# Two 3x3 convolutions behind an attention layer: input channels in two row halves of the array, each half summed in a PSUM bank of its own

## The chip, the cores and the metric

One core of a Trainium2 chip runs the kernel. The metric is the device time of one execution in microseconds (us). The kernel before takes 2547.97 us, the median of four runs (2547.29 to 2551.29).

## What is computed

The input `x` is float32 of shape (4, 128, 64, 64): four images of 128 channels. Two layers follow each other. The first is a group norm, a self-attention with four heads of 32 over the 4096 positions of an image, a projection and a residual. The second, which the change touches, is a block of two quantized 3x3 convolutions, each with batch-norm statistics over all images:

```python
def conv3x3_decomposed(x, wq):
    xp = jnp.pad(x, ((0, 0), (0, 0), (1, 1), (1, 1)))
    out = jnp.zeros((B, wq.shape[0], H, W), dtype=x.dtype)
    for kh in range(3):
        for kw in range(3):
            out = out + jnp.einsum('bchw,oc->bohw', xp[:, :, kh:kh + H, kw:kw + W], wq[:, :, kh, kw])
    return out
...
residual = x
out = conv3x3_decomposed(x, lsq_quantize(w1, alpha1))
out = jax.nn.relu(batchnorm(out, gamma1, beta1))
out = conv3x3_decomposed(out, lsq_quantize(w2, alpha2))
out = batchnorm(out, gamma2, beta2)
out = jax.nn.relu(out + residual)
```

Both convolutions have 128 input and 128 output channels, so one tap of one block of positions is one product of a 128x128 weight with a 128-row operand. The mean and variance of the batch norm run over all 4 x 4096 positions of a channel. The second convolution can therefore start only when the first is finished for all images.

## The kernel before

**Stages.** The attention comes first and fills about 2235 us. In it, TensorE works in bursts of three score pairs (line 442) and three weight halves (line 456), ScalarE takes the exponentials (line 444) and VectorE adds up rows (line 471). Its scores are products over 64 rows: `k[r, half, ...]` against `q[r, half, part, :]` with `r` the lower or upper 64 partitions, and the two halves go to two banks of one PSUM tile (lines 439 to 443). Then come the two convolution layers (`layer`, called in lines 885 and 939) and a closing pass that adds the residual and stores the output (lines 940 to 951).

**Bands and chunks.** An image is cut into four bands of 16 rows, which makes 16 bands for four images (`bandlist`). A band has two chunks `j` of 8 rows, that is of 512 positions, which is one PSUM bank of float32. A band's input is held three times in SBUF, padded to 18 rows of 66: `t` in float32, `hi` rounded to the fast format fp32r, and `lo`, the rest. `split` (lines 570 to 575) makes `hi` with a VectorE cast and `lo` with a VectorE subtraction. In the second layer `relu_band` (lines 898 to 903) does this after ScalarE has applied batch norm and ReLU. All come from one ring of nine buffers (`kpool`).

**One chunk.** `conv` (lines 775 to 785) issues 18 matmuls into one bank: 9 taps over `hi`, then 9 over `lo`, each with the full 128x128 weight of the tap and a moving operand of 8 rows of 64.

**PSUM.** `conv_tile` takes a tile of two banks from `pss`, a ring of three such tiles that the attention's scores also use; here one tile holds the two chunks of a band. The two remaining banks are the pool `psa`.

**Order of the work.** The order on each engine is the order of the program's text (`manual_schedule`). The first two bands of the first layer are convolved at the attention's end, among its last steps, into the tiles `early` (lines 791 to 803). `layer` (lines 834 to 861) then goes over the bands but the last: convolve both chunks, call `prepare(m)`, which prepares band m + 2 (and loads band m + 3 in the first layer), then for each chunk run `bn_stats` on VectorE and a copy on ScalarE, both reading the bank. At m = 5 of the first layer, `prepare` also counts bad values with one small matmul. The last band's chunks go to banks of `psa`; while TensorE works on them, VectorE aggregates the statistics of all other chunks (line 850), and ten small matmuls (`keep_warm`) close the layer.

Of the kernel before, what the change touches and what calls it, by code (L numbers as in the profile page):

```python
# [16 lines left out]
F32 = mybir.dt.float32  # L17
AF = mybir.ActivationFunctionType
ALU = mybir.AluOpType
# [3 lines left out]
P = 128  # L23
# [3 lines left out]
TAPS = 9  # L27
FB = 512
# [50 lines left out]
def _fast_body(ctx, tc, x, norm_w, norm_b, qkv_wt, qkv_b, proj_wt, proj_b,  # L79
               w1, alpha1, gamma1, beta1, w2, alpha2, gamma2, beta2, out, cnt):  # L80
    nc = tc.nc
    B, C, H, W = x.shape
    assert C == P and W == 64
    N = H * W
    RB = FB // W
    NB = N // FB
# [52 lines left out]
    wq = [const.tile([P, TAPS, P], F32R, name="wq0")]  # L139
# [69 lines left out]
    pss = ctx.enter_context(tc.tile_pool(name="pss", bufs=3, space=PSUM))  # L209
# [96 lines left out]
    def keep_warm(count):  # L306

        t = psa.tile([P, FB], F32, name=f"idle{count}", tag="a")
        for _ in range(count):
            nc.tensor.matmul(t[:, 0:P], gavg, gavg, start=True, stop=True)  # L310
# [266 lines left out]
    raw, ready = {}, {}  # L577
# [17 lines left out]
    st = small.tile([P, NB, 6], F32, name="st0", tag="st")  # L595
# [144 lines left out]
    todo, parts = [], {}  # L740
# [34 lines left out]
    def conv(parts, ps, j, w):  # L775
        hi, lo = parts
        r0 = j * RB
        n = 0
        for part in (hi, lo):
            for tap in range(TAPS):  # L780
                kh, kw = divmod(tap, 3)
                nc.tensor.matmul(ps.rearrange("p (r w) -> p r w", w=W), w[:, tap, :],  # L782
                                 part[:, r0 + kh : r0 + kh + RB, kw : kw + W],
                                 start=(n == 0), stop=(n == 2 * TAPS - 1))
                n += 1

    def conv_tile(i, b, g):
        return pss.tile([P, 2, FB], F32, name=f"c{i}_{b}_{g}", tag="s")


    early = [conv_tile(0, *bandlist[m]) for m in range(2)]
    last = parts[len(blocks) - 1]
    conv(ready[0, 0, 0], early[0][:, 0, :], 0, wq[0])
# [13 lines left out]
    cv = [mid.tile([P, N], F32, name=f"cv{b}") for b in range(B)]  # L807
# [11 lines left out]
    def batch_norm(i, st):  # L819

        mv = small.tile([P, 2], F32, name=f"bmv{i}", tag="mv")
        nc.vector.bn_aggr(mv, st)
        r = small.tile([P, 1], F32, name=f"br{i}", tag="rs")
        nc.vector.tensor_scalar(r, mv[:, 1:2], a_q[i], EPS, ALU.mult, ALU.add)
        nc.gpsimd.tensor_tensor(r, r, mhalf, ALU.pow)
        na = small.tile([P, 1], F32, name=f"bn{i}", tag="dv")
        nc.vector.tensor_tensor(na, r, a_n[i], ALU.mult)
        c = small.tile([P, 1], F32, name=f"bc{i}", tag="gc")
        nc.vector.scalar_tensor_tensor(c, mv[:, 0:1], na, bn[i][1], ALU.mult, ALU.add)
        a = small.tile([P, 1], F32, name=f"ba{i}", tag="ga")  # L830
        nc.vector.tensor_tensor(a, r, a_g[i], ALU.mult)
        return a, c

    def layer(i, prepare, done):


        st = mid.tile([P, B * NB, 6], F32, name=f"st{i}")
        end = mid.tile([P, 15], F32, name=f"end{i}")
        nc.gpsimd.memset(end[:, 0:1], float((B * NB - 2) * FB))
        for m, (b, g) in enumerate(bandlist[:-1]):  # L840
            ps = done[m] if m < len(done) else conv_tile(i, b, g)
            for j in range(2):
                if m >= len(done):
                    conv(ready[i, b, g], ps[:, j, :], j, wq[i])
            prepare(m)
            for j in range(2):
                c = 2 * g + j
                nc.vector.bn_stats(st[:, b * NB + c, :], ps[:, j, :])  # L848
                nc.scalar.copy(cv[b][:, c * FB : (c + 1) * FB], ps[:, j, :])  # L849
        nc.vector.bn_aggr(end[:, 1:3], st.rearrange("p j s -> p (j s)")[:, : 6 * B * NB - 12])  # L850
        nc.vector.tensor_scalar(end[:, 2:3], end[:, 2:3], float((B * NB - 2) * FB), None, ALU.mult)
        b, g = bandlist[-1]
        for j in range(2):
            ps = psa.tile([P, FB], F32, name=f"c{i}_last{j}", tag="a")
            conv(ready[i, b, g], ps, j, wq[i])
            c = 2 * g + j
            nc.vector.bn_stats(end[:, 3 + 6 * j : 9 + 6 * j], ps)
            nc.scalar.copy(cv[b][:, c * FB : (c + 1) * FB], ps)
        prepare(len(bandlist) - 1)
        keep_warm(10)  # L860
        return batch_norm(i, end)
# [11 lines left out]
    def first(m):  # L873
# [8 lines left out]
        if m + 2 < len(bandlist) and m > 0:  # L882
            split_band(*bandlist[m + 2])

    a1, c1 = layer(0, first, early)

    def relu_rows(b, g, t, r0, r1):
# [45 lines left out]
    def second(m):  # L933
        if m + 2 < len(bandlist):
            relu_band(*bandlist[m + 2])
        if m < 4 * B - 4:
            load_res(m // 4, m % 4)

    a2, c2 = layer(1, second, [])
    for i in range(4):  # L940
        load_res(B - 1, i)
    for b in range(B):
        for j in range(4):
            for p in range(2 if b == j == 0 else 1):
                n = HN // 2 if b == j == 0 else HN
                y = res[b, j][:, p * n : (p + 1) * n]
# [464 lines left out]
```

## Time and profile before

| | us |
|---|---|
| median of four runs | 2547.97 |
| the profiled execution | 2549.55 |
| its span (first to last instruction) | 2547.8 |
| TensorE busy (share of the span) | 2508.6 (98%) |
| VectorE busy | 2137.4 (84%) |
| ScalarE busy | 2087.4 (82%) |
| copy of a chunk, `cv<-c`, line 849, 128x512 | 0.587 each, 60 of them |
| `bn_stats` of a chunk, line 848, 128x512 | 0.699 each, 60 of them |
| cast to `hi`, line 573, 128x1188 | 0.764 each |
| subtraction to `lo`, line 574, 128x1188 | 1.396 each |
| sum of a PSUM and an SBUF operand, `kst<-pk,b,kst`, line 352, 128x512 | 0.751 each |

All times below are of one profiled execution, counted from its first instruction. A group of instructions is named by its line, engine, operation and tiles (out<-in). Matmuls are pipelined: the duration of one (about 0.4 us) is longer than the distance from its start to the next start, so a rate is read from starts, not from durations.

### The profile page before, as it was taken

To read this page: it belongs to the slowest core of one execution; us is meant where nothing else is said; L and a number is where in the kernel's file an instruction comes from. 1 tells how busy PE (TensorE), PEld (TensorE's weight loads), DVE (VectorE), ACT (ScalarE), POOL (GpSimd) and SP (SyncE) were. 2 spreads that over 40 slices of the span, in tenths; PEclk is the share of its full clock that TensorE was granted. 3 is DMA by queue.
4 is the path that set the end of the run, shared out by engine and by line. 5 is a ranking of instruction groups with operands and counts; after the bars stand their busy time and mean duration, and the time that the engine had idled before them with its cause. 6 is when DMAs were issued, how large, how long until landed. Compare 5 with 4: busy or idle time off the path is not lost.

```text
span 2547.8 us, 65043 instructions
## 1 busy us (share of the span) xinstructions
PE 2508.6 (98%) x28708; PEld 1505.6 (59%) x28708; DVE 2137.4 (84%) x1402; ACT 2087.4 (82%) x2278; POOL 281.6 (11%) x461
## 2 busy tenths in 40 slices
PE   9999999999999999999999999999999999999995
PEld 6555555555555555555555555555555555577774
DVE  6899888889988889889988888889999999954445
ACT  5998888999988999999988899989999999911224
POOL 2111111111011111110111111111000011000000
PEclk9999999999999999999999999999999999999998
DMA  6877667787757667797766666796666666645004
GB/s 196 190 185 171 166 171 183 174 203 177 184 132 191 168 153 171 164 230 163 172 164 171 158 165 157 191 201 152 149 138 144 146 144 152 148 89 160 1 1 166
DMA packets 148955, 403.86 MB, mean 159 GB/s; under 512 B 59417, under 2 KB 60185, under 8 KB 120121
## 3 DMA queue, kind: packets, MB, share of 16 engines
q0 software_dynamic: 45840, 280.39, 48.2%
q1 hardware_dynamic: 100952, 113.60, 16.9%
q8 instruction: 227, 3.72, 0.6%
q10 hardware_dynamic: 1872, 5.64, 0.6%
q14 instruction: 64, 0.52, 0.1%
HBM read 107.48 MB, written 56.42 MB: 64 GB/s over the span
## 4 chain that ended last, share of the span: by engine, by line
PE 70%; issue 3%; DMA 2%; DVE 1%; ACT 1%; POOL 0%; ACTq 0%; POOLq 0%; DVEq 0%
PE s L442 31%; PE acc L456 27%; PE c L782 9%; DMA rm<-p 2%; PE l L488 1%; PE po L317 1%; PE pk L317 1%; PE pq L317 1%; PE pv L317 1%; DVE r L471 0%; ACT res L949 0%; ACT p L444 0%; PE c_last L782 0%; DVE r L469 0%; DVE res L948 0%
## 5 line engine op out<-in xcount | busy, mean ns | idle before, releaser
L444 ACT ACTIVATE p<-s 128x1024 f32<-128x1024 f32 x2048 | 1950.6, 1032 | 202.8 <-PE s L442 154.2
L471 DVE TENSOR_TENSOR r<-r,p 128x2048 f32<-128x2048 f32 x768 | 1758.3, 2289 | 65.2 <-ACT p L444 14.8
L442 PE MATMUL s<-q,k 64*128 64x512 f32 x8192 | 1139.7, 410 | 2.0 <-ACT p L444 1.6
L456 PE MATMUL acc<-p,v 128*32 128x256 f32 x16384 | 1026.4, 383 | 0.0
L442 PEld LDWEIGHTS s<-q,k 64*128 64x128 f32 x8192 | 717.0, 185 | 409.9 <-issue 166.9
L456 PEld LDWEIGHTS acc<-p,v 128*32 128x32 f32 x16384 | 463.7, 109 | 482.3 <-issue 247.7
L466 POOL DMA_DIRECT2D rm<-p x160 | 139.5, 872 | 803.6 <-ACT p L444 555.0
L849 ACT COPY cv<-c 128x512 f32<-128x512 f32 x60 | 35.2, 587 | 200.1 <-DVE st L848 200.1
L782 PE MATMUL c<-hi,wq 128*128 128x512 f32 x540 | 139.1, 402 | 1.3 <-issue 1.3
L782 PE MATMUL c<-lo,wq 128*128 128x512 f32 x540 | 138.5, 401 | 0.0
L848 DVE BATCH_NORM_STATS2 st<-c 128x6 f32<-128x512 f32 x60 | 41.9, 699 | 104.0 <-PE c L782 83.4
L782 PEld LDWEIGHTS c<-hi,wq 128*128 128x128 f32 x540 | 101.3, 188 | 30.2 <-issue 2.1
L782 PEld LDWEIGHTS c<-lo,wq 128*128 128x128 f32 x540 | 101.8, 188 | 27.1
L352 DVE SCALAR_TENSOR_TENSOR kst<-pk,b,kst 128x512 fp32r<-128x512 f32 x32 | 24.0, 751 | 83.4 <-PE s L442 68.5
L469 DVE TENSOR_TENSOR r<-p,p 128x2048 f32<-128x2048 f32 x32 | 73.2, 2289 | 12.9 <-ACT p L444 12.9
L352 DVE SCALAR_TENSOR_TENSOR qst<-pq,b,qst 128x512 fp32r<-128x512 f32 x32 | 24.0, 751 | 58.4 <-PE s L442 47.4
L356 POOL DMA_DIRECT2D qd<-qst x31 | 23.6, 761 | 265.6 <-DVE qst L352 223.8
L492 POOL DMA_DIRECT2D r<-rm x31 | 26.2, 844 | 219.3 <-DMA rm<-p 88.7
L356 POOL DMA_DIRECT2D kd<-kst x27 | 20.0, 740 | 175.6 <-DVE kst L352 162.4
L488 PE MATMUL l<-r,ones 128*32 128x256 f32 (+1 forms) x504 | 37.7, 382 | 0.0
L464 POOL DMA_DIRECT2D rm<-p x32 | 17.8, 557 | 178.7 <-ACT p L444 80.4
L351 ACT ACTIVATE kst<-pk,b 128x512 fp32r<-128x512 f32 x32 | 22.3, 699 | 17.8 <-PE pk L317 17.7
(149 smaller groups left out, 736.6 us busy)
## 6 DMA issues: line engine op xcount, KB each, us to landing
rm<-p POOLq DMA_DIRECT2D x192, 1024.0 KB, 7.8
q<-qd SPq DMA_DIRECT2D x248, 128.0 KB
r<-rm POOLq DMA_DIRECT2D x31, 1024.0 KB, 8.0
x<-in_x_dram SPq DMA_DIRECT2D x86, 256.0 KB
k<-kd SPq DMA_DIRECT2D x124, 128.0 KB
qd<-qst POOLq DMA_DIRECT2D x31, 512.0 KB, 5.8
kd<-kst POOLq DMA_DIRECT2D x27, 512.0 KB, 5.0
y<-x POOLq DMA_DIRECT2D x32, 256.0 KB, 6.6
```

Source lines behind the costliest of these rows:

```text
L317: nc.tensor.matmul(out[cs, :], w[:, cs], x, start=True, stop=True)
L352: nc.vector.scalar_tensor_tensor(lo, ps[what], bias, t[:, 0, :], ALU.add, ALU.subtract)
L356: (nc.sync if start else nc.gpsimd).dma_start(out=dst[b, j].rearrange("s p n -> p s n"), in_=t)
L442: nc.tensor.matmul(s[:, i, :], k[r, half, c0 : c0 + P], q[r, half, part, :], start=(part == 0), stop=(part == 1))
L444: nc.scalar.activation(pts[step][:, 2 * half : 2 * half + 2, :], s, AF.Exp, scale=SCALE)
L456: nc.tensor.matmul(acc[n][h * D : (h + 1) * D, cs], v[:, kt % KB, h * D : (h + 1) * D], pt[:, h, cs], start=(kt == 0 and half == 0), stop= ...
L466: nc.gpsimd.dma_start(out=msum[n], in_=pt, accum_op=ALU.add)
L469: nc.vector.tensor_tensor(rsum[n], pts[step - 1], pt, ALU.add)
L471: nc.vector.tensor_tensor(rsum[n], rsum[n], pt, ALU.add)
L488: nc.tensor.matmul(t["l"][h * D : (h + 1) * D, cs], ones, r[:, h, cs], start=first, stop=end)
L782: nc.tensor.matmul(ps.rearrange("p (r w) -> p r w", w=W), w[:, tap, :], part[:, r0 + kh : r0 + kh + RB, kw : kw + W], start=(n == 0), stop ...
L848: nc.vector.bn_stats(st[:, b * NB + c, :], ps[:, j, :])
```

## The change

All chunks except those of the first two bands of the first layer and those of the last band of each layer use a new function `conv_apart`. For each tap of `hi` and of `lo` it issues two matmuls in place of one: channels 0 to 63 into the first bank of the tile, channels 64 to 127 into the second. A tile of two banks thus holds one chunk, where it held the two of a band. After a chunk, ScalarE copies the first bank to SBUF, VectorE adds the second bank to the copy in place, and `bn_stats` reads the sum from SBUF. A chunk's evacuation is issued directly behind the chunk, and `prepare(m)` stands behind the second chunk's matmuls and ahead of its evacuation.

```diff
-    def conv_tile(i, b, g):
-        return pss.tile([P, 2, FB], F32, name=f"c{i}_{b}_{g}", tag="s")
+    def conv_apart(parts, ps, j, w):
+        r0 = j * RB
+        n = 0
+        for part in parts:
+            for tap in range(TAPS):
+                kh, kw = divmod(tap, 3)
+                for i in range(2):
+                    r = slice(i * P // 2, (i + 1) * P // 2)
+                    nc.tensor.matmul(ps[:, i, :].rearrange("p (r w) -> p r w", w=W), w[r, tap, :],
+                                     part[r, r0 + kh : r0 + kh + RB, kw : kw + W],
+                                     start=(n == 0), stop=(n == 2 * TAPS - 1))
+                n += 1
+
+    def conv_tile(i, b, g, j=""):
+        return pss.tile([P, 2, FB], F32, name=f"c{i}_{b}_{g}{j}", tag="s")
...
         for m, (b, g) in enumerate(bandlist[:-1]):
-            ps = done[m] if m < len(done) else conv_tile(i, b, g)
-            for j in range(2):
-                if m >= len(done):
-                    conv(ready[i, b, g], ps[:, j, :], j, wq[i])
-            prepare(m)
+            if m < len(done):
+                prepare(m)
             for j in range(2):
                 c = 2 * g + j
-                nc.vector.bn_stats(st[:, b * NB + c, :], ps[:, j, :])
-                nc.scalar.copy(cv[b][:, c * FB : (c + 1) * FB], ps[:, j, :])
+                y = cv[b][:, c * FB : (c + 1) * FB]
+                if m < len(done):
+                    nc.vector.bn_stats(st[:, b * NB + c, :], done[m][:, j, :])
+                    nc.scalar.copy(y, done[m][:, j, :])
+                    continue
+                ps = conv_tile(i, b, g, j)
+                conv_apart(ready[i, b, g], ps, j, wq[i])
+                if j == 1:
+                    prepare(m)
+                nc.scalar.copy(y, ps[:, 0, :])
+                nc.vector.tensor_tensor(y, y, ps[:, 1, :], ALU.add)
+                nc.vector.bn_stats(st[:, b * NB + c, :], y)
```

## The prediction, made before the changed kernel was run

> **What bounds the kernel now.** I read the page's chain first, then the busy time by stage, then the order of single instructions in a convolution stage, and last the attention's scores, because these already have the form that the change gives the convolutions. The chain of waits, in order of time, from the last part of the first layer to the closing pass:
>
> ```profile
> 2289.87 43.16 PE c L782 x180
> ...
> 2379.53 129.03 PE c L782 x540
> 2508.56 8.60 PE c_last L782 x36
> ```
>
> 540 matmuls in 129.03 us are 0.2389 us each, with nothing between them. The single starts in the trace say the same: 238.6 ns from start to start over 1142 neighbours, and by tap 236 to 241 ns. The stages by engine (columns: length, then busy time with counts of PE, weight loads, VectorE, ScalarE, POOL; clock):
>
> ```profile
> 2256.00:2378.00 122.00, 122.00 (x524) 96.54 (x522) 53.91 (x78) 18.78 (x32) 3.73 (x36) 1.00 0.42 111
> 2378.00:2519.00 141.00, 139.68 (x597) 110.63 (x597) 58.40 (x71) 40.19 (x51) 3.77 (x44) 1.00 0.05 15
> ```
>
> TensorE is full in both layers at a clock of 1.00; VectorE stands at 44% and 41%. So the layers are worth what a tap costs TensorE, plus whatever makes it wait. The timeline at the first layer's start, where the ring of PSUM tiles is tightest:
>
> ```profile
> 2258.86 0.70 DVE L848 BATCH_NORM_STATS2 st<-c 128x6 f32<-128x512 f32 x1 [0.60 <-DMA y<-x]
> ...
> 2259.53 2.31 PE L782 MATMUL c<-hi,wq 128*128 128x512 f32 x9
> 2259.64 0.59 ACT L849 COPY cv<-c 128x512 f32<-128x512 f32 x1 [13.57 <-DVE st L848]
> ...
> 2260.99 0.59 ACT L849 COPY cv<-c 128x512 f32<-128x512 f32 x1 [0.77 <-DVE st L848]
> ...
> 2265.11 0.59 ACT L849 COPY cv<-c 128x512 f32<-128x512 f32 x1 [0.77 <-DVE st L848]
> ```
>
> The first early tile is free at 2260.99 + 0.59 = 2261.58, the second at 2265.70; their evacuation began only at 2258.86, behind a store of the attention's. The matmul line at 2259.53 begins the second chunk of the third band. The scores, TensorE alone, in one burst (four of the six pairs by themselves, from narrow cuts of the timeline, and the next group):
>
> ```profile
> 1201.93 0.39 PE L442 MATMUL s<-q,k 64*128 64x512 f32 x2
> ...
> 1202.16 0.39 PE L442 MATMUL s<-q,k 64*128 64x512 f32 x2
> ...
> 1202.39 0.40 PE L442 MATMUL s<-q,k 64*128 64x512 f32 x2
> ...
> 1202.62 0.40 PE L442 MATMUL s<-q,k 64*128 64x512 f32 x2
> ...
> 1202.95 0.42 PE L456 MATMUL acc<-p,v 128*32 128x256 f32 x4
> ```
>
> Two matmuls of 64 rows start together (3 ns apart, median), and pairs follow every 0.23 us: 232.4 ns, mean over some 2,700 undisturbed pairs.
>
> **What the Trainium skill says.** "TensorEngine Tiling (Array Packing)", Key Properties, says that row tiles run weight loads and matmuls independently and that changing the tiling mode drains TensorE. The trace agrees: the 64-row weight loads also start 3 ns apart, each 185 ns, and the last pair ahead of the 32-column group is followed after 323 ns instead of 232. "TensorE: Matmul & The Clock Gate", Why this matters for your kernels, says that a product over few rows takes the same time as one over 128, so that only concurrency gains: here 392 ns against 401 for one matmul. "PSUM — Partial Sum Buffer", Specifications, says that a VectorE instruction takes at most one tensor input from PSUM, which is why a copy must come ahead of the sum; no such pair of inputs is in the trace.
>
> **The change part by part.**
>
> *The tap.* 13 bands of the first layer and 15 of the second, 2 chunks each, 18 taps: 28 x 36 = 1008 full matmuls become 1008 pairs. The array does the same work, since both halves of its rows were busy already. The trace lacks a 64-row pair whose moving operand is 8 rows of 64 out of 66; scores stream 512 contiguous elements. Nearest rows: the pair at 232.4, the full tap at 238.6. If the 6.2 ns come from the tiling, a pair costs 232.4 and the change gains 1008 x 6.2 = 6.2 us. If they come from the operand's rows, it stays at 238.6 and gains nothing. A loss is not excluded: two streams with row breaks might each pay the 6.2 ns, giving 232.4 + 12.4 = 244.8 and 1008 x 6.2 = 6.2 us lost. The 5 ns spread between taps, whose addresses differ while their shape does not, says that the operand's layout matters. So I take 237, near the full tap: 1008 x -1.6 = -1.6 us.
>
> *Twice the weight loads.* 1008 more, 64 rows each. In the scores, two of them lie beside each other under the previous pair and the rate holds over a burst, so I cost them at nothing beyond the pair. Were the two of a tap one after the other, the 185 ns of the second would show: 1008 x 0.185 = 186 us.
>
> *The mode.* Only the passages to the last band of each layer are new switches; the others stood beside 32-column work already. Leaving the scores costs 323 - 232 = 91 ns, and the second pair after a switch comes at 337 instead of 232, 105 more. Two switches x 0.196 = 0.4 us.
>
> *The ring.* A tile now holds one chunk, so three chunks of 4.3 us are in flight instead of three bands. The third band's first chunk takes the free tile; its second needs the first early tile. TensorE gets there at 2259.53, and the tile is free at 2261.58. With 0.06 us of signal (ScalarE's first `hi` ends at 2379.44, the load that waited starts at 2379.50) it restarts at 2261.64: 2.1 us of waiting, and 0.1 for refilling after it. The evacuations ahead are in the same order as before, so this doesn't move. The next chunk needs the second early tile at 2261.64 + 4.3 = 2265.9, which is free at 2265.70, so no second wait. Before, the tile was needed only at 2263.58. The sum of the ring is 2.2 us. If the pause also lowered the clock for a while, up to 2 us would come on top; after the 1.3 us pause ahead of 2379.53 the nine matmuls took 2.39 us against 2.31, so I take nothing.
>
> *The evacuation.* Per chunk, ScalarE's copy (0.587) no longer waits for `bn_stats`; VectorE's sum of a PSUM and an SBUF operand is new, nearest row line 352 at 0.751, bounds 0.69 (line 537, SBUF only) and 0.75; `bn_stats` now reads SBUF, 0.699 from PSUM, taken as the same. VectorE per band of 8.6 us: 2 x (0.75 + 0.70) + 0.76 + 1.40 = 5.1 us against 3.6, which is 59% and no bound. From a chunk's end: copy to 0.6, sum to 1.4, `bn_stats` to 2.1 us; both banks are free after 1.4 us and wanted after two further chunks, 8.6 us. With that cover gone each chunk would show 1.4 us, 56 x 1.4 = 78 us.
>
> *What is moved.* `prepare(m)` now queues behind the first chunk's sum and `bn_stats` on VectorE, and in the second layer its ReLU (1.30) behind a copy on ScalarE. Both wait for the end of the first chunk. Behind the waiting sum stand the cast and the subtraction for band m + 2: ReLU done at 2.0 us after that end, cast 2.9, subtraction 4.3, and band m + 2 starts 12.9 us after it. The DMAs that `prepare` issues (band m + 3, the weights, the residuals) keep their place on SP's queue, and the border memsets theirs on POOL's; neither waits for the new sum. The second chunk's sum queues behind the subtraction, ending at the time its matmuls end. Ahead of the layer's last band, copy, sum, `bn_stats` and aggregation (0.6 + 0.75 + 0.7 + 1.1) are over 3.2 us after the last tiled chunk, and VectorE is wanted 4.3 us after it. The layer's end, batch norm and closing pass don't change. All of this costs nothing.
>
> *Sum.* -1.6 + 0.4 + 2.2 = +1.0 us: the profiled execution's span of 2547.8 becomes 2548.8, its own 2549.55 becomes 2550.6; on the median of 2547.97 that is 2549.0. What can be told from no change is 0.2%, that is 5.1 us.
>
> **The rivals.**
>
> *A, the forecast, 0.48:* a pair costs 235 to 241, the sum is -1.0 to +5.0 us, 2547 to 2553; 2549.0 at 237.
>
> *B, the pair keeps the scores' rate, 0.17:* 232.4 gives -6.2 + 2.6 = -3.6, 2544.3 us. For it: the same form in some 2,700 pairs. Against it: the contiguous operand. Only below 231 ns, or with the ring's wait absent, does it pass 0.2%: 0.06 of its chance.
>
> *C, row breaks of two streams add up, 0.30:* a pair takes 244.8 in all 1008 taps, +6.2 + 2.6 = +8.8, 2556.8 us. It decides from 241.1 ns on, where 1008 x 2.5 ns + 2.6 reaches 5.1 us. For it: full taps with rows are slower than contiguous pairs, and two streams have twice the breaks. Against it: the streams read different partitions and start together.
>
> *D, the halves don't run beside each other, 0.05:* the change would not do what it says; the second half's load shows, +186 + 2.6, 2737 us. The scores' 3 ns speak against it.
>
> **How the numbers follow.** A and the slow part of B, 0.48 + 0.11, are no change: 0.59. Faster is B's 0.06, slower C and D: 0.35. The likeliest case is A: 2549.0. The range runs from 2543.5, which leaves out B's edge (0.05), to 2558, which leaves out D and C's upper third (0.15).
>
> **What would show it.** Pair starts near 237 ns, 127 to 130 us for the 540 tiled taps of the second layer; a TensorE idle of about 2.1 us at 2259.5 that ends with ScalarE's copy of the second early chunk, and none after it; no other VectorE or ScalarE release of a convolution; VectorE near 59% in both layers. The forecast is wrong if pairs leave 231 to 241, if TensorE waits for sums or copies of later chunks, or if the first early tile is free sooner.

## The result, and the profile after

The changed kernel takes 2550.85 us (median of 32 runs) against 2548.17 us of the kernel before (52 runs). The ratio is 1.001, with a 95% interval of 1.0005 to 1.0015, so the change costs 2.7 us, where the interval allows 1.3 to 3.8. The forecast was 1.0 us more, in a range that holds the measured time. The profiled execution has a span of 2549.4 us; before, it was 2547.8.

The chain of waits of the changed kernel, in order of time (start, length, what):

```profile
2255.50 2.30 DMA y<-x
2258.02 0.71 DVE st L862
2258.80 0.59 ACT cv L863
2259.41 0.71 DVE st L862
2260.15 0.59 ACT cv L863
2260.78 30.30 PE c L797 x252
...
2380.99 129.04 PE c L797 x1080
2510.03 8.80 PE c_last L782 x36
```

Two things are to be seen. The 540 taps of the second layer, now 1080 matmuls, take 129.04 us; before, 540 took 129.03. And the chain, which ran through TensorE alone at the first layer's start, now comes through a store (`y<-x`), the statistics and the copies of the first early tile. The timeline at that place, first of the kernel before, from the third band's first chunk to the fourth band's:

```profile
2255.14 2.41 PE L782 MATMUL c<-hi,wq 128*128 128x512 f32 x9
...
2263.82 2.31 PE L782 MATMUL c<-hi,wq 128*128 128x512 f32 x9
```

Then of the changed kernel, over the same stretch:

```profile
2254.30 2.41 PE L797 MATMUL c<-hi,wq 64*128 64x512 f32 x18
...
2256.56 2.31 PE L797 MATMUL c<-lo,wq 64*128 64x512 f32 x18
...
2258.02 0.70 DVE L862 BATCH_NORM_STATS2 st<-c 128x6 f32<-128x512 f32 x1 [0.60 <-DMA y<-x]
...
2260.15 0.58 ACT L863 COPY cv<-c 128x512 f32<-128x512 f32 x1 [0.77 <-DVE st L862]
2260.78 1.96 PEld L797 LDWEIGHTS c<-hi,wq 64*128 64x128 f32 x18 [2.37 <-ACT cv L863]
2260.78 2.41 PE L797 MATMUL c<-hi,wq 64*128 64x512 f32 x18 [1.92 <-ACT cv L863]
...
2265.17 2.31 PE L797 MATMUL c<-hi,wq 64*128 64x512 f32 x18
```

The third band's second chunk would follow 18 taps and one refill after 2254.30, that is at 2254.30 + 0.1 + 18 x 0.2385 = 2258.69. It starts at 2260.78, 0.05 us after ScalarE's copy ends. TensorE loses 2.09 us there, once. (The 1.92 us of idle that the line shows count from the modelled end of the matmul before.) From the third band to the fourth it is 10.87 us, where the kernel before takes 8.68: the 2.09 of waiting and 0.10 of refilling after it. The waits of both layers hold no other of TensorE's on an evacuation. Its one other wait there, 1.3 us ahead of the second layer, is in the kernel before too (us in total, times, longest):

```profile
ACT cv L869 <- PE c L797: 180.9, 54, 4.0
...
DVE cv L870 <- ACT cv L869: 94.7, 51, 2.9
...
PE c L797 <- ACT cv L863: 1.9, 1, 1.9
...
PE c L797 <- issue: 1.3, 1, 1.3
```

The new sums and statistics on VectorE, from the page, and the two stages by engine:

```profile
L870 DVE TENSOR_TENSOR cv<-cv,c 128x512 f32<-128x512 f32 x56 | 38.5, 688 | 94.9 <-ACT cv L869 94.7
...
L871 DVE BATCH_NORM_STATS2 st<-cv 128x6 f32<-128x512 f32 x56 | 38.9, 695 | 1.9
```

```profile
2256.00:2378.00 122.00, 120.08 (x971) 94.19 (x968) 70.17 (x98) 18.09 (x31) 2.53 (x32) 1.00 0.42 112
2378.00:2519.00 141.00, 139.69 (x1136) 124.80 (x1135) 77.21 (x102) 40.18 (x51) 3.93 (x45) 1.00 0.05 16
```

VectorE goes from 53.91 to 70.17 us and from 58.40 to 77.21 us, which is 58% and 55% of the stages. It has become busier by 35 us in the two layers, and none of it is on the path.

The whole account, from the timelines (first row) and the chains:

| place | before | after | difference |
|---|---|---|---|
| third band of the first layer begins | 2255.14 | 2254.30 | -0.84 |
| second layer begins | 2379.53 | 2380.99 | +1.46 |
| its last band begins | 2508.56 | 2510.03 | +1.47 |
| its last statistics begin | 2517.18 | 2518.86 | +1.68 |

The attention happened to end 0.84 us earlier in this execution. From there to the second layer the changed kernel loses 2.30 us: 2.19 at the ring, and 0.11 for the passage from pairs to the whole taps of the last band, less what the pairs gain. By single starts, the two steps at this passage take 326 and 346 ns in place of 239, which is 0.2 us, and the pairs' slightly shorter steps give back about 0.1. The second layer with its own passage costs another 0.22 (1.68 - 1.46). The sum is 2.5 us, where the medians say 2.7.

### The profile page after: what moved, and what is told of

Its sections match the earlier page's. It is cut to its first block, busy times and chain, and to the rows that moved or that the text cites. A ratio compares the mean times of both kernels' runs of the same rounds, so it can differ in the third digit from the quotient of the medians.

```text
span 2549.4 us, 67122 instructions
## 1 busy us (share of the span) xinstructions
PE 2510.8 (98%) x29716; PEld 1521.7 (60%) x29716; DVE 2174.2 (85%) x1458; ACT 2087.2 (82%) x2278; POOL 281.8 (11%) x461
## 4 chain that ended last, share of the span: by engine, by line
PE 69%; issue 3%; DMA 3%; ACT 1%; DVE 1%; SPq 0%; ACTq 0%; POOL 0%; POOLq 0%; DVEq 0%
PE s L442 30%; PE acc L456 27%; PE c L797 8%; DMA rm<-p 2%; PE l L488 1%; PE po L317 1%; ACT p L444 1%; DMA rc<-rd 1%; PE pk L317 1%; PE pv L317 1%; PE pq L317 1%; ACT res L971 0%; PE c_last L782 0%; DMA q<-qd 0%; DVE r L471 0%
## 5 line engine op out<-in xcount | busy, mean ns | idle before, releaser
L797 PE MATMUL c<-hi,wq 64*128 64x512 f32 x1008 | 130.4, 398 | 3.2 <-ACT cv L863 1.9
L797 PE MATMUL c<-lo,wq 64*128 64x512 f32 x1008 | 130.1, 398 | 0.0
L870 DVE TENSOR_TENSOR cv<-cv,c 128x512 f32<-128x512 f32 x56 | 38.5, 688 | 94.9 <-ACT cv L869 94.7
L797 PEld LDWEIGHTS c<-hi,wq 64*128 64x128 f32 x1008 | 101.8, 185 | 22.4 <-ACT cv L863 2.4
L797 PEld LDWEIGHTS c<-lo,wq 64*128 64x128 f32 x1008 | 102.2, 185 | 18.1
L871 DVE BATCH_NORM_STATS2 st<-cv 128x6 f32<-128x512 f32 x56 | 38.9, 695 | 1.9
```

Source lines behind the costliest of these rows:

```text
L797: nc.tensor.matmul(ps[:, i, :].rearrange("p (r w) -> p r w", w=W), w[r, tap, :], part[r, r0 + kh : r0 + kh + RB, kw : kw + W], start=(n == ...
L871: nc.vector.bn_stats(st[:, b * NB + c, :], y)
```

## The experiments

### What the wait at the ring is worth

The third band goes back to whole taps, with both of its chunks in one tile. TensorE then needs the early tiles one band later.

```diff
         for m, (b, g) in enumerate(bandlist[:-1]):
+            if i == 0 and m == 2:
+                done.append(conv_tile(i, b, g))
+                for j in range(2):
+                    conv(ready[i, b, g], done[m][:, j, :], j, wq[i])
```

> The changed kernel with the third band of the first layer convolved whole again (full 128-row taps, both chunks in one tile); all else as changed. Theory (the ring's wait is most of the loss): TensorE no longer waits at the early tiles, so the 2.1 us wait goes and one more mode switch (0.2 us) comes; about 1.9 us less than the changed kernel, within 1 us of the kernel before, and no idle of TensorE between 2255 and 2290 us. Rival (the loss is spread over the pairs or the sums): the time stays within 0.5 us of the changed kernel.

Measured: 2548.02 us against 2547.9 of the kernel before, ratio 1.0 with an interval of 0.9992 to 1.0009. That is within 1 us of the kernel before, as the theory says; the rival, a time near the changed kernel's, falls. TensorE's timeline has no gap at the place:

```profile
2251.14 2.41 PE L782 MATMUL c<-hi,wq 128*128 128x512 f32 x9
2253.39 2.30 PE L782 MATMUL c<-lo,wq 128*128 128x512 f32 x9
2255.53 2.31 PE L782 MATMUL c<-hi,wq 128*128 128x512 f32 x9
2257.68 2.31 PE L782 MATMUL c<-lo,wq 128*128 128x512 f32 x9
2259.92 2.40 PE L797 MATMUL c<-hi,wq 64*128 64x512 f32 x18
```

The chunks' groups of nine taps start 2.1 to 2.3 us apart throughout. From the third band to the second layer it is 2251.14 to 2375.88, 124.74 us, where the kernel before takes 124.39 and the changed one 126.69. The 0.35 left over is near the 0.4 us of two passages between tilings. To time the two versions beside each other, both ran again on one chip.

> The changed kernel itself, timed beside the next run on the same chip. Theory (the sum of the ring's wait and two switches): 2.5 us over the kernel before. Rival (no difference that lasts): within 1 us of it.

> The changed kernel with the third band whole, again, beside the changed kernel on the same chip. Theory (the ring's wait): 1.9 us less than the changed kernel, 0.6 us over the kernel before, which are its three switches of 0.2 us. Rival (the loss is elsewhere): the changed kernel's time.

Measured: the changed kernel 2550.68, ratio 1.0011 (1.0002 to 1.0019); the one with the third band whole 2548.5, ratio 1.0003 (0.9995 to 1.0012); before 2547.66. The changed kernel is 3.0 us over the kernel before (2.5 were expected) and the other 0.8 (0.6 expected); the difference of the medians is 2.2 us, near the wait of 2.09. The means of the two sets of 13 runs differ by 1.8 us, with a 95% interval of 0.7 to 2.9 (resampled from these runs), so the direction is clear and the size is not. The traces give the size. This second execution of the changed kernel waits at the same place, for the same copy:

```profile
2259.84 2.41 PE L797 MATMUL c<-hi,wq 64*128 64x512 f32 x18 [1.93 <-ACT cv L863]
```

From its third band to its fourth it takes 10.88 us, and with the third band whole 8.78 in both executions. The one wait was nearly all of the loss. Whether the switches of 0.2 us are all of the rest is too small for the times.

### What sets the rate of a tap

The forecast left open whether the scores' faster rate (232.4 ns against 238.6) came from their tiling or from their contiguous operand. Two experiments give the convolutions a contiguous operand, once in pairs and once in whole taps.

```diff
+    def moving(part, rows, r0, kh, kw):
+        s = (r0 + kh) * PW + kw
+        return part.rearrange("p r w -> p (r w)")[rows, s : s + FB]
...
-                    nc.tensor.matmul(ps[:, i, :].rearrange("p (r w) -> p r w", w=W), w[r, tap, :],
-                                     part[r, r0 + kh : r0 + kh + RB, kw : kw + W],
+                    nc.tensor.matmul(ps[:, i, :], w[r, tap, :],
+                                     moving(part, r, r0, kh, kw),
```

The edit of the whole taps is the same, in `conv`.

> The changed kernel, but each pair streams 512 contiguous elements from the same start instead of 8 rows of 64 out of 66 (so it convolves other positions; full taps of the early and last bands as before). Theory (the rows of the moving operand cost the 6.2 ns): pairs at 232.4 ns, as the scores, in both layers: 1008 x 6.0 ns = 6.0 us less of TensorE time than the changed kernel. Rival (something else in the convolution, such as the weights or the long run of pairs, holds it at 238.5): pairs stay at 238.5.

> The kernel before, with full 128-row taps that stream 512 contiguous elements from the same start (other positions than the reference's). Theory (rows of the operand): 232.4 ns a tap, so the tiling plays no part in the rate; 1152 x 6.2 ns = 7.1 us less than the kernel before. Rival (128 rows against 64 make the difference): 238.6 ns a tap still, and the time of the kernel before.

The second layer in the two chains, the pairs and then the whole taps:

```profile
2377.42 125.91 PE c L801 x1080
```

```profile
2374.49 126.15 PE c L786 x540
```

By single starts, pairs take 232.8 ns and whole taps 233.0, near the 232.4 of both theories. The times are 2544.8 and 2541.39 us, one run each, where runs of the kernel before spread over 2546.5 to 2551.5. 1152 taps at 5.6 ns less are 6.5 us, which is also what the second one gains on 2547.9. So the tiling plays no part in the rate. The access pattern of the moving operand does, and it costs a pair the same as one whole tap. (The edit also writes the bank as one stretch in place of 8 rows of 64, the same 512 elements. That this is not the cause is seen below, where taps that write 8 rows reach 234 ns.)

A run of the operand is a stretch of it that lies together in SBUF. The next two experiments change the number of these runs, in whole taps on the kernel before; one computes four, the other sixteen, as the comments added here say.

```diff
-                                 part[:, r0 + kh : r0 + kh + RB, kw : kw + W],
+                                 moving(part, slice(0, P), r0, kh, kw),
...
+    def moving(part, rows, r0, kh, kw):      # four runs of 128
+        wide = part.rearrange("p (r s) w -> p r (s w)", s=2)
+        a = r0 // 2 + kh // 2
+        return wide[rows, a : a + 4, kw : kw + 2 * W]
...
+    def moving(part, rows, r0, kh, kw):      # sixteen runs of 32
+        return part[rows, kh : kh + 16, kw : kw + W // 2]
```

> The kernel before, with full taps that stream 4 runs of 128 elements, 132 apart, instead of 8 of 64 (other positions than the reference's). Theory (each break in the stream costs the same): from 233.0 ns at one run and 238.6 at eight, 0.8 ns a break, so 3 breaks give 235.4 ns a tap. Rival (any stream that isn't contiguous costs one fixed sum): 238.6 ns.

> The kernel before, with full taps that stream 16 runs of 32 elements, 66 apart (other positions than the reference's). Theory (each break costs 0.8 ns): 233.0 + 15 x 0.8 = 245.0 ns a tap, about 7 us more than the kernel before over 1152 taps. Rival (one fixed sum): 238.6 ns and the time of the kernel before.

Measured: 237.4 ns with four runs and 249.7 with sixteen, 2547.12 and 2563.93 us, one run of each kernel. Neither expectation holds. Four runs cost more than three equal breaks, and sixteen more than fifteen. Sorted by tap, the four-run taps are not alike: 234 ns where `kw` is 0, and 239 where it is 1 or 2. With a row pair of 132 elements, all runs of a `kw = 0` tap start on a multiple of 16 bytes, counted from the buffer's start. This led to an experiment with rows of 68 elements, where the same holds for runs of 64. (Rows of 72 elements, which would start on multiples of 32 bytes, did not fit into SBUF, so they have no time.)

```diff
-    PW = W + 2
+    PW = W + 4
...
-        nc.gpsimd.memset(f32(t)[:, :, W + 1 : W + 2], 0.0)
+        nc.gpsimd.memset(f32(t)[:, :, W + 1 : PW], 0.0)
```

> The kernel before with rows of 68 elements in place of 66 in the convolutions' buffers (the added columns are zero and no tap reads them), so that every row starts on a multiple of 16 bytes. Theory (where a run starts decides: with four runs the taps at kw = 0 took 234 ns and those one and two elements further 239): taps at kw = 0 near 234, the others near 239 to 241, about 237.5 on average, 1 to 1.5 us less than the kernel before. Rival (the number of runs decides): 238.6 for all, the time of the kernel before.

Measured: 2551.06 us against 2547.35 of the kernel before, ratio 1.0014 (1.0007 to 1.002), slower. The mean tap takes 241.2 ns; 1152 taps at 2.6 ns more are 3.0 us of the 3.7. By the single starts, in ns to the next start (mean over the three `kh`):

| runs of the operand | kw = 0 | kw = 1 | kw = 2 |
|---|---|---|---|
| 1 of 512, rows of 66 | 233 | 234 | 232 |
| 4 of 128, 132 apart | 234 | 239 | 239 |
| 8 of 64, 66 apart (kernel before) | 238 | 239 | 239 |
| 8 of 64, 68 apart | 234 | 240 | 250 |
| 16 of 32, 66 apart | 249 | 250 | 250 |

Where all runs start on 16 bytes, four or eight runs are within 1 ns of one contiguous stretch, so breaks alone cost at most that. With eight runs, 68 apart, starts 4 bytes off cost 6 ns and starts 8 bytes off 16 ns. The expectation was right for `kw` of 0 and 1 and wrong for 2, and that one tap in three made the kernel slower. Where the runs don't all start on 16 bytes, their number and length count too: eight runs of 64 and sixteen of 32, both 66 apart, start at the same offsets from 16 bytes, and take 238 to 239 ns and 249 to 250.

A contiguous operand takes 232 to 234 ns at any `kw`, so a start costs only where there are breaks. There is no fixed price per start. In the kernel before, every second run of a `kw = 0` or `kw = 2` tap starts 8 bytes off; halfway between 234 and 250 would be 242 ns, and 238 to 239 are measured. Why 8 bytes cost more with eight runs 68 apart than with four runs or with eight 66 apart stays open. The starts are counted within the buffer; the traces show no addresses. A layout in which only offsets of 0, 4 and 12 bytes occur was not tried. By the fastest rate measured, at most 6.5 us can be gained in the two layers.

### What the order beside each other is worth

Here the two halves of a chunk come one after the other.

```diff
-        n = 0
-        for part in parts:
-            for tap in range(TAPS):
-                kh, kw = divmod(tap, 3)
-                for i in range(2):
-                    r = slice(i * P // 2, (i + 1) * P // 2)
+        for i in range(2):
+            r = slice(i * P // 2, (i + 1) * P // 2)
+            n = 0
+            for part in parts:
+                for tap in range(TAPS):
+                    kh, kw = divmod(tap, 3)
...
-                n += 1
+                    n += 1
```

> The changed kernel with the order of one chunk's matmuls turned: 18 taps of channels 0 to 63 first, then 18 of channels 64 to 127, same banks, same sums. Theory (a half costs TensorE as much as a full tap, and only the order beside each other hides the second): 1008 more steps of 238.5 ns, 240 us more, less the ring's 2.1 us. Rival (the queue brings the halves together by itself): the changed kernel's time within 10 us.

Measured: 2695.53 us in one run, 147.6 more than the kernel before, which lies between the two expectations. The chain gives the second layer's 1080 matmuls:

```profile
2446.25 208.21 PE c L797 x1080
```

That is 6.94 us a chunk: more than the 4.30 of halves beside each other, less than the 36 x 0.2385 = 8.59 of halves in turn. TensorE's timeline over one turn shows why:

```profile
2500.30 1.58 PE L797 MATMUL c<-lo,wq 64*128 64x512 f32 x6
2501.49 0.50 PE L797 MATMUL c<-hi,wq 64*128 64x512 f32 x1
2501.72 0.40 PE L797 MATMUL c<-lo,wq 64*128 64x512 f32 x1
2501.83 0.40 PE L797 MATMUL c<-hi,wq 64*128 64x512 f32 x1
2501.96 0.40 PE L797 MATMUL c<-lo,wq 64*128 64x512 f32 x1
2502.07 0.40 PE L797 MATMUL c<-hi,wq 64*128 64x512 f32 x1
2502.20 0.40 PE L797 MATMUL c<-lo,wq 64*128 64x512 f32 x1
2502.32 1.58 PE L797 MATMUL c<-hi,wq 64*128 64x512 f32 x6
```

Inside a half, matmuls start 0.24 us apart. Where one half ends (its `lo` taps), matmuls of the next half (its `hi` taps) start among the last ones of it, 0.12 us apart, over 0.8 us. A chunk has two such turns, one between its halves and one to the next chunk, and about 7 of its 36 steps are hidden in this way (36 - 6.94 / 0.2385). In this kernel halves come together by themselves over a short stretch only; for all of a chunk they have to be written side by side. What limits the stretch was not looked into.

## Why the prediction was right, and where its sizes were off

**The tap.** The forecast put a pair at 237 ns, 1.6 us gained over 1008 pairs. Measured is 238.44, where the whole tap takes 238.57: 0.1 us gained. This term is the one that was mis-sized: 1.5 us of the 1.7 between +1.0 and +2.7. The reason given was right (the operand's layout, not the tiling), and if it had been followed to its end the price would have been 238.6; the 237 was a hedge towards the scores' rate, which no row with this operand supported. In the profiled execution the pairs even repeat the whole taps' pattern tap by tap (240.8 ns at the second tap against 241.1).

**Rival B**, the scores' rate, falls: it takes a contiguous operand, which the pairs of the changed kernel don't have. **Rival C**, row breaks of two streams that add up to 244.8 ns, falls too: the breaks cost a pair no more than a whole tap. **Rival D**, halves that don't run beside each other, falls: the two of a pair start 3 to 30 ns apart. It priced that case at 186 us; halves written in turn lost 148.

**The ring.** Predicted 2.1 us of waiting from 2259.53 to 2261.64, and 0.1 for refilling; measured 2.09 and 0.10, at the tile and behind the copy that were named, and 0.86 us earlier because the attention ended earlier in this execution. The forecast also named 2 us for a lower clock after the pause, with no measured number behind them, and then took nothing. That was right: the granted clock of the stage is 1.00, and the first nine taps after the pause take 2.41 us, as the nine at 2254.30 do, which no such pause precedes. No second wait followed: the next chunk's tile was free at 2264.27 + 0.59 = 2264.86, and TensorE came for it at 2265.17. This was a close thing, a margin of 0.3 us where 0.2 was forecast.

**The mode.** Predicted 0.4 us for two switches of 0.196; by single starts, the first layer's took 0.20 and the second's 0.23.

**The evacuation and the moved preparation.** Predicted to be hidden, and it was: VectorE at 58% and 55% against 59% forecast, the sum 0.688 us against 0.75. No wait of TensorE on a sum is in the trace. So the ring, the mode and the hidden work were forecast for the right reasons, and no two errors cancelled; the one error lay in the tap, and the range, laid around it for the tap's sake, had room for it.

## What to carry to other kernels

Splitting the contraction into two row halves gives the array nothing when all its rows are busy already; the second bank and the sum stayed hidden here, but the buffers that the change takes from a ring showed at the place where the ring was tightest. So look at who holds the ring's slots when a stage begins, not at the steady state. And when a nearby row has the right form but another access pattern, take the price from the row with the same pattern.

## What was not expected of the hardware

- Where the runs of the moving operand start changes the rate of a 512-column fp32r matmul: with eight runs of 64, 68 apart, 234 ns with all starts on 16 bytes of the buffer, 240 at 4 bytes off, 250 at 8 bytes off. With starts on 16 bytes, breaks in the operand cost no more than 1 ns (234 ns with four and eight runs, 233 for a contiguous operand).
- With the halves in turn, the first matmuls on the other half of the rows start ahead of the last ones that stand before them in the program (2501.49 against 2502.20 us): 0.12 us apart at the turn, about 7 of 36 steps.
- The two matmuls of a pair start 3 ns apart in the first layer, and 30 ns apart in the second (17 and 37 in other executions), at the same rate of 238.4 to 238.8 ns. What sets this offset was not looked into.
